# Attention's first pair: value gathers and next tables behind the rotations, and ScalarE for the roots of the first rotations

## The chip, the cores and the metric

The kernel runs on one core of a Trainium2 chip. The metric is the device time of one execution in microseconds (us). The kernel before takes 3504.65 us, the median of 3 runs (3504.32 to 3507.08). In the profile, PE is TensorE's matrix work, PEld its weight loads, DVE is VectorE, ACT is ScalarE, POOL is GpSimd, and SP is the engine from whose queue most DMAs start.

## The reference, cut to what matters

The program is a network of four stages over 64 sequences of 32 tokens with 512 features, in float32: 2048 rows, which the kernel holds as 16 tiles of 128 rows. Each stage adds its result to `x`. The change lies in the third, an attention with cached keys and values (32 query heads, 8 key heads, 128 features per head, pages of 32 positions, 16 pages per sequence):

```python
def _rmsnorm(t, w):
    var = jnp.mean(t * t, axis=-1, keepdims=True)
    return t * jax.lax.rsqrt(var + EPS) * w

def _rope(t, pos):
    ...
    t1, t2 = (t[..., :D // 2], t[..., D // 2:])
    return jnp.concatenate([t1 * cos - t2 * sin, t2 * cos + t1 * sin], axis=-1)
```

For each token, `x` is multiplied by `Wq`, `Wk` and `Wv`; the heads of q and k go through `_rmsnorm` and `_rope`; the scores of q against the 512 cached keys and the sequence's own 32 are masked by the sequence's length, put through a softmax and multiplied with the values; `Wo` brings the result back to 512 features. What the change touches is the norm's factor `rsqrt(mean(t*t) + EPS)` and the rotation of the first tiles, and the order in which cached values are fetched.

## The kernel before, in words

**Steps and pairs.** Attention (`attention`, from line 1015) goes in 32 steps: two halves of the heads (16 query heads and 4 key heads each), and 16 tiles in each half. Two steps make a pair, whose two tiles are projected together (`class Projections`), so there are 16 pairs. Of a pair there are three groups of products: g = 0 gives keys and values, g = 1 and 2 the queries. A group is 7 products of half the depth (`ORDER`, a scheme of Strassen's kind: sums of quarter blocks of `x` in `x_sums`, prepared sums of the weights), each accumulated in one of two PSUM buffers (`mm`). After products 1 and 5 of a group ScalarE copies the buffer out (line 1212); after the others VectorE adds it to a result (line 1220; lines 1222 and 1225 add once more). A buffer is free for the next product but one when that is done.

**A rotation.** Every finished key or query tile (128 rows x 4 heads x 128) goes through `rotated` (line 1123). ScalarE squares it (L1116), VectorE sums the squares (L1118) and scales the sums (L1119), GpSimd raises them to the power -0.5 (L130) into `rs`. Meanwhile VectorE writes the products of the swapped halves with the sine table into `swapped`, of which there are two buffers (L1130), and multiplies the tile by the cosine table (L1133). GpSimd adds the two (L1134), which frees the `swapped` buffer, and multiplies with `rs` (L1135). TensorE then transposes the tile (`turned`, L1055) through a single PSUM buffer `tq`, and ScalarE copies the transposed keys (`kT_own`, L1234) or queries (`qT`, L1238) out. I call the rotations of the first pair k0, k1, q0, q1 and so on, in the order of the work.

**Tables.** The cosine and sine tables are already multiplied with the norm's weight: `tables` (line 1168) has GpSimd make two products for each of the two tiles (L1173), so four for the keys and four for the queries of a pair.

**Scores and values.** For a sequence and a key head, TensorE makes the scores (L1342), VectorE masks them and finds the largest (L1347), ScalarE takes the exponential (L1349), VectorE the reciprocal of its sum (L1351), ScalarE scales the part of the own positions (L1352), VectorE the rest (L1354); TensorE transposes the weights (L1055), ScalarE copies them (L1360), and TensorE multiplies with the values (L1060, `po`). The cached values come in `load_values` (line 1083): four gathers on GpSimd's queue, of 128 rows of 2 KB each. Own values are copied by ScalarE, eight small copies for two sequences (L1093). Key pages and weights are ordered by SP, in a fixed order (`load_by`, line 99).

**What sets the order.** The order within a pair is written out by hand as 64 slots for `turned`, `product`, `tables`, `x_sums` and so on. Pair n calls the key tables of pair n+2 in slot 40, and the query tables of pair n+1 in slot 3. In the first pair the tables of the second pair are called in slots 7 and 10. Ahead of the first slot stands a prologue (lines 1461 to 1514), which does the first 21 products of pair 0 in portions, `products(4)`, `products(5)` and so on, with the key loads, own values, the gathers of the first sequences (`values_of(0)` and `values_of(HKP)`) and the first transposes between. A framework places each engine's instructions in a queue by priorities and data, so an instruction that has its data early can be moved ahead of others; `tc.issue_after(ins)` forces those issued inside it to stand behind `ins` on their engine. In the prologue of before, the gathers are forced to stand behind `p.last_pool`, the last of pair 0's own table products.

Of the kernel before, what the change touches and what calls it, by code (L numbers as in the profile page):

```python
# [27 lines left out]
AF = mybir.ActivationFunctionType  # L28
ALU = mybir.AluOpType
# [4 lines left out]
P = 128  # L34
# [9 lines left out]
HQ, HK, HD = 32, 8, 128  # L44
# [5 lines left out]
REP = HQ // HK  # L50
# [964 lines left out]
def attention(c, known, x_in, y_part, y_out, sums, tail):  # L1015
# [15 lines left out]
    tc, nc, a = c.tc, c.nc, c.a  # L1031
    half = HD // 2
    n_c = L // P
    with ExitStack() as outer:
# [8 lines left out]
        cos, sin, rows, lens = known.cos, known.sin, known.rows, known.lens  # L1043
        norm, keys = known.norm, known.keys
# [52 lines left out]
        soon = []  # L1097
# [22 lines left out]
            c.inverse_root(rs, REP)  # L1120
            return rs

        def rotated(t, tab):

            src = t.rearrange("p (h d) -> p h d", d=HD)
            ct, st = tab
            rs = squares_and_root(src)
            tmp = wk.tile([P, REP, HD], F32, name="swapped", bufs=2)
            for lo, hi in ((0, half), (half, 0)):
                nc.vector.tensor_tensor(  # L1130
                    tmp[:, :, lo:lo + half], src[:, :, hi:hi + half],
                    st[:, lo:lo + half].unsqueeze(1).to_broadcast([P, REP, half]), ALU.mult)
            nc.vector.tensor_tensor(src, src, ct.unsqueeze(1).to_broadcast([P, REP, HD]), ALU.mult)  # L1133
            nc.gpsimd.tensor_tensor(src, src, tmp, ALU.add)  # L1134
            nc.gpsimd.tensor_tensor(src, src, rs.unsqueeze(2).to_broadcast([P, REP, HD]), ALU.mult)  # L1135

        K2 = KC // 2

# [15 lines left out]
        class Projections:  # L1154
# [13 lines left out]
            def tables(self, n):  # L1168
                for i, T in enumerate(self.T):
                    ct = qp.tile([P, 2, half], F32, name=n + "_cos")  # L1170
                    st = qp.tile([P, 2, half], F32, name=n + "_sin")
                    for t, w_n, f in ((ct, norm[n][0], cos), (st, norm[n][1], sin)):
                        self.last_pool = nc.gpsimd.tensor_tensor(  # L1173
                            t, w_n, f[:, T, :].unsqueeze(1).to_broadcast([P, 2, half]), ALU.mult).ins
                    self.tabs[n, i] = tuple(t.rearrange("p u f -> p (u f)") for t in (ct, st))

            def x(self, i):
# [23 lines left out]
            def product(self, g, m):  # L1201
                (x11, x12), (_, x22) = self.blocks
                lhs = {1: x11, 2: x12, 3: self.s[3], 4: x22, 5: self.s[0], 6: self.s[1], 7: self.s[2]}[m]
                w = wps.pop(0)
                acc = ps.tile([P, D], F32, tag="mm", bufs=2, name="pq" if g else "pkv")
                part(acc, [(lhs[:, k, :], w[:, k, :]) for k in range(K2)], True, True)

                d = self.d = {} if m == 1 else self.d
                if m in (1, 5):
                    at = (0, 1) if m == 1 else (1, 1)  # L1210
                    d[at] = self.place(g, *at)
                    nc.scalar.copy(d[at], acc)
                    return
                if m == 2:
                    d[0, 0] = self.place(g, 0, 0)
                elif m == 6:
                    d[1, 0] = self.place(g, 1, 0)
                to, other = {2: ((0, 0), (0, 1)), 6: ((1, 0), (0, 1)), 3: ((0, 1), (1, 0)),
                             7: ((1, 0), (1, 0)), 4: ((1, 0), (1, 0))}[m]
                nc.vector.tensor_tensor(d[to], acc, d[other], ALU.add)  # L1220
                if m == 3:
                    nc.vector.tensor_tensor(d[0, 1], d[0, 1], d[1, 1], ALU.add)
                elif m == 7:
                    to = (1, 1)
                    nc.vector.tensor_tensor(d[1, 1], d[1, 1], d[1, 0], ALU.add)
                if m != 6 and not (g == 0 and to[1]):
                    soon.append(partial(rotated, d[to], self.tabs["q" if g else "k", to[0]]))

            def turned(self, g, i, n):
                r = self.c.pop((g, i, n)).rearrange("p (h d) -> p h d", d=HD)  # L1230
# [183 lines left out]
        projections = [Projections(n) for n in range(len(steps) // 2)]  # L1414
# [9 lines left out]
        def values_of(i):  # L1424
            if i < len(turns):
                s, h, b, _ = of(i)
                load_values(h, b)
# [33 lines left out]
        p = projections[0]  # L1461
# [11 lines left out]
        def products(n):  # L1473

            for i in range(count[0], count[0] + n):
                p.product(i // 7, p.ORDER[i % 7])
                if i >= 7 and p.ORDER[i % 7] in (7, 4):
                    held.extend(soon)
                    del soon[:]
                the_rest()  # L1480
                if i < 3 * 7 - 8 or i >= 3 * 7 - 4:
                    next_wp()
            count[0] += n
# [6 lines left out]
        for i in (0, HKP):  # L1490
            own_values_of(i)
        products(5)
        with tc.issue_after(p.last_pool):
            values_of(0)
        new_keys(0, 1)
        p.turned(0, 0, 0)
        load_keys(0, 1, range(2))
# [2 lines left out]
        p.turned(0, 1, 0)  # L1500
        products(1)
        p.turned(1, 0, 0)
        products(1)
        load_keys(0, 1, range(2, 4))
        start(0)
# [1 line left out]
        p.turned(1, 0, 1)  # L1507
        products(2)
        start(1)
        with tc.issue_after(p.last_pool):  # L1510
            values_of(HKP)
        projections[1].load()
        products(1)
# [12 lines left out]
        for s, (h, T) in enumerate(steps):  # L1526
# [3 lines left out]
            n = s // 2  # L1530
# [599 lines left out]
```

## Time and profile before

| what | value |
|---|---|
| time, median of 3 runs | 3504.65 us (3504.32 to 3507.08) |
| the profiled execution's own time | 3513.04 us |
| its span on the core | 3511.2 us |
| granted TensorE clock, mean | 0.991 |
| TensorE time in 1200 to 3160 us | 1957.04 of 1960 us |
| L1134, GpSimd add in the rotation | 160 times, 1301 ns each |
| L130, GpSimd power | 160 times, 1125 ns each |
| L1135, GpSimd product with the root | 160 times, 1078 ns each |
| L1086, gathers on GpSimd's queue | 512 times, 1009 ns each |
| L1173, table products on GpSimd | 128 times, 0.44 to 0.97 us each |

The profile is of one execution. Its times run from the start of the span; attention's first products start shortly before 1000 us, its first slots at about 1042 us, and after the first pairs one pair takes about 142 us. A line of a timeline gives the start, the duration, the engine and line, what is written and read, and in brackets how long the engine was idle before and what ended that. In a table of windows each column is an engine's busy time in the stretch, then the granted clock of TensorE (1.00 is full speed), the share of the DMA engines' time and the GB/s.

### The profile page before, as it was taken

The numbers are of one execution on the slowest core, as the hardware profiler recorded it, in microseconds if no ns is written. First come the engines' busy times: TensorE is split into PE (matmuls) and PEld (weight loads), VectorE is DVE, ScalarE is ACT, GpSimd is POOL, SyncE is SP. The second block draws the span as 40 slices with busy tenths as digits, with TensorE's granted clock in tenths as the row PEclk, the third lists the DMA queues.
The fourth block names the chain that finished last, engine by engine and source line by source line (L and its number), as shares of the span: only waits on it lengthen the run. The fifth ranks groups of instructions, "written<-read, shape, count | busy, mean of one in ns | idle before, by whom it ended". The sixth has DMA issues, their size and how long they took to land. (4 is left out here: it accounts for less than half of the span.)

```text
span 3511.2 us, 66971 instructions
## 1 busy us (share of the span) xinstructions
PE 3429.1 (98%) x21124; PEld 2690.3 (77%) x21124; DVE 2186.3 (62%) x5429; ACT 1627.0 (46%) x4259; POOL 1650.5 (47%) x1650
## 2 busy tenths in 40 slices
PE   8999999999989999999999999999999999999988
PEld 6556888888857777778777787787777877778776
DVE  5454444444357676776766767767677676675555
ACT  5332222222226555555555555555555555556322
POOL 0112433333257565655646556556565574554222
PEclk9999999999999999999999999999999999999989
DMA  5013645454467778788887888878878888878511
GB/s 207 25 52 125 195 154 176 156 165 154 142 225 233 238 258 260 251 261 252 258 260 251 253 257 255 264 245 262 268 250 269 257 262 263 255 235 250 187 59 43
DMA packets 631936, 740.26 MB, mean 211 GB/s; under 512 B 64546, under 2 KB 480290, under 8 KB 631586
## 3 DMA queue, kind: packets, MB, share of 16 engines
q1 hardware_dynamic: 580130, 562.94, 51.3%
q0 software_dynamic: 51456, 173.05, 14.1%
q8 instruction: 171, 2.80, 0.3%
q14 instruction: 179, 1.47, 0.1%
HBM read 689.61 MB, written 46.14 MB: 210 GB/s over the span
## 5 line engine op out<-in xcount | busy, mean ns | idle before, releaser
L1086 POOL DMA_INDIRECT vt<-in_v_rows,v_rows x512 | 516.4, 1009 | 300.9 <-PE po L1060 175.6
L1349 ACT ACTIVATE pr<-pr,low 128x544 f32<-128x544 f32 x512 | 383.3, 749 | 546.9 <-DVE low L1347 544.9
L1342 PE MATMUL sc<-kt,qT 128*128 128x288 f32 (+1 forms) x2048 | 554.7, 393 | 8.7 <-DVE low L1347 5.4
L1342 PEld LDWEIGHTS sc<-kt,qT 128*128 128x128 f32 x2048 | 384.9, 190 | 223.7 <-issue 121.0
L1060 PEld LDWEIGHTS po<-prT,vt 128*128 128x128 f32 x4096 | 522.7, 192 | 33.4 <-ACT prT L1360 13.8
L1060 PE MATMUL po<-prT,vt 128*128 128x128 f32 x4096 | 544.3, 276 | 3.5 <-ACT prT L1360 2.0
L1347 DVE CUSTOM_DVE_ANT_0 pr<-sc,mask 128x544 f32<-128x544 f32 x512 | 368.1, 719 | 140.7 <-PE sc L1342 140.1
L1134 POOL TENSOR_TENSOR projected<-projected,swapped 128x512 f32<-128x512 f32 x160 | 208.2, 1301 | 303.1 <-DVE projected L1133 278.3
L1354 DVE TENSOR_SCALAR pr<-pr,low 128x512 f32<-128x512 f32 x512 | 317.1, 619 | 12.8
L1055 PE MATMUL prT_ps<-ident,pr 128*128 128x128 f32 x2048 | 312.1, 275 | 1.6 <-DVE pr L1354 1.5
L1360 ACT COPY prT<-prT_ps 128x512 f32<-128x512 f32 x512 | 294.0, 574 | 32.6 <-PE prT_ps L1055 25.2
L1351 DVE RECIPROCAL low<-low 128x1 f32<-128x1 f32 x512 | 81.9, 160 | 318.4 <-ACT pr L1349 318.0
L1055 PEld LDWEIGHTS prT_ps<-ident,pr 128*128 128x128 f32 x2048 | 237.7, 142 | 10.9 <-issue 2.9
L1060 PE MATMUL py<-wo,oT 128*128 128x256 f32 x1024 | 243.5, 381 | 0.0
L1060 PE MATMUL pq<-wp,x_sums 128*128 128x512 f32 x512 | 240.5, 593 | 0.1
L1060 PEld LDWEIGHTS py<-wo,oT 128*128 128x128 f32 x1024 | 187.5, 191 | 21.5
L130 POOL TENSOR_TENSOR rs<-rs,minus_half 128x4 f32<-128x4 f32 x160 | 180.0, 1125 | 22.2 <-DVE low L1351 14.6
L1060 PE MATMUL pq<-wp,xT 128*128 128x512 f32 x384 | 183.7, 602 | 5.0 <-DVE projected L1220 5.0
L1060 PE MATMUL py<-wo,o_sum 128*128 128x256 f32 x768 | 182.9, 382 | 3.0 <-DVE o_sum L1278 2.1
L1352 ACT ACTIVATE own_pr<-pr,low 128x32 f32<-128x32 f32 x512 | 164.9, 322 | 44.1 <-DVE low L1351 41.0
L1093 ACT COPY own_vt<-v 32x128 f32<-32x128 f32 x512 | 150.8, 295 | 55.1 <-PE po L1060 42.4
L1135 POOL TENSOR_TENSOR projected<-projected,rs 128x512 f32<-128x512 f32 x160 | 172.6, 1078 | 7.9
(348 smaller groups left out, 6477.6 us busy)
## 6 DMA issues: line engine op xcount, KB each, us to landing
kt<-in_kT SPq DMA_DIRECT2D x2048, 64.0 KB
wp<-in_sums SPq DMA_DIRECT2D x192, 512.0 KB
wo<-out_sums SPq DMA_DIRECT2D x128, 512.0 KB
wp<-in_WqT SPq DMA_DIRECT2D x96, 512.0 KB
wo<-in_WoT SPq DMA_DIRECT2D x96, 512.0 KB
down1T<-in_down1T SPq DMA_DIRECT2D x80, 256.0 KB
wp<-in_WkT SPq DMA_DIRECT2D x32, 512.0 KB
xt<-x SPq DMA_DIRECT2D x48, 256.0 KB
```

The lines of the kernel that those rows point to most:

```text
L130: self.nc.gpsimd.tensor_tensor(t, t, self.minus_half[:, :n], ALU.pow)
L1055: c.on_pe(nc.tensor.transpose(pt[:, m, :], piece, c.ident))
L1060: c.on_pe(nc.tensor.matmul(out, lhsT, rhs, start=first and i == 0, stop=last and i == len(pairs) - 1))
L1086: nc.gpsimd.indirect_dma_start(out=vts[b % 2][:, n, :], out_offset=None, in_=a["v_rows"], in_offset=bass.IndirectOffsetOnAxis(ap=rows[h][: ...
L1134: nc.gpsimd.tensor_tensor(src, src, tmp, ALU.add)
L1135: nc.gpsimd.tensor_tensor(src, src, rs.unsqueeze(2).to_broadcast([P, REP, HD]), ALU.mult)
L1342: c.on_pe(nc.tensor.matmul(sc[:, lo + n * PSIZE:lo + m * PSIZE].rearrange("p (n k) -> p n k", k=PSIZE), q, kt[:, n:m, g, :], start=True, s ...
L1347: nc.vector.tensor_tensor_reduce(pr[:, :NK], sc[:, lo:lo + NK], masks[h, b], -SCALE, 3.0e38, ALU.add, ALU.min, low[:, 0:1])
L1349: nc.scalar.activation(pr[:, :NK], pr[:, :NK], AF.Exp, bias=low[:, 0:1], scale=-1.0, accum_out=low[:, 1:2])
L1352: nc.scalar.activation(own_prs[b % 2][:, g * S:(g + 1) * S], pr[:, L:NK], AF.Copy, scale=low[:, 2:3])
L1354: nc.vector.tensor_scalar(pr[:, :L], pr[:, :L], low[:, 2:3], None, ALU.mult)
L1360: last_prT.append(nc.scalar.copy(prT, pt).ins)
```

## The change

The change has four parts, all in `attention`:

1. `rotated` keeps the instruction of its GpSimd add (L1134 of before) in a list `last_turn`.
2. It gets a switch `by_scalar`. With it, the product with the root is done by ScalarE, in four products of 128x128, one for each head, instead of one GpSimd product of 128x512. It is set in the first pair alone, for the keys' two rotations and the first two of the queries, four in all.
3. `tables` no longer records `last_pool`. Its products are forced to stand behind the last L1134 that was written so far, if there is one. This holds for the tables of all pairs but the first.
4. In the prologue the first gathers, `values_of(0)`, move from after 14 products to behind the third transpose, and are forced to stand behind the last L1134 so far, the fifth of the pair, instead of behind pair 0's tables. The gathers of the second sequence, `values_of(HKP)`, stay in their place in the code, and are forced to stand behind the last L1134 there, the sixth.

```diff
+        last_turn = []
+
-        def rotated(t, tab):
+        def rotated(t, tab, by_scalar=False):
...
-            nc.gpsimd.tensor_tensor(src, src, tmp, ALU.add)
-            nc.gpsimd.tensor_tensor(src, src, rs.unsqueeze(2).to_broadcast([P, REP, HD]), ALU.mult)
+            last_turn.append(nc.gpsimd.tensor_tensor(src, src, tmp, ALU.add).ins)
+            if by_scalar:
+                for h in range(REP):
+                    nc.scalar.activation(src[:, h, :], src[:, h, :], AF.Copy, scale=rs[:, h:h + 1])
+            else:
+                nc.gpsimd.tensor_tensor(src, src, rs.unsqueeze(2).to_broadcast([P, REP, HD]), ALU.mult)
...
-                    for t, w_n, f in ((ct, norm[n][0], cos), (st, norm[n][1], sin)):
-                        self.last_pool = nc.gpsimd.tensor_tensor(
-                            t, w_n, f[:, T, :].unsqueeze(1).to_broadcast([P, 2, half]), ALU.mult).ins
+                    with tc.issue_after(last_turn[-1]) if last_turn else nullcontext():
+                        for t, w_n, f in ((ct, norm[n][0], cos), (st, norm[n][1], sin)):
+                            nc.gpsimd.tensor_tensor(
+                                t, w_n, f[:, T, :].unsqueeze(1).to_broadcast([P, 2, half]), ALU.mult)
...
-                    soon.append(partial(rotated, d[to], self.tabs["q" if g else "k", to[0]]))
+                    soon.append(partial(rotated, d[to], self.tabs["q" if g else "k", to[0]],
+                                        self is projections[0] and (g == 0 or g == 1 and m in (2, 3))))
...
         products(5)
-        with tc.issue_after(p.last_pool):
-            values_of(0)
         new_keys(0, 1)
...
         p.turned(1, 0, 0)
+        with tc.issue_after(last_turn[-1]):
+            values_of(0)
         products(1)
...
-        with tc.issue_after(p.last_pool):
+        with tc.issue_after(last_turn[-1]):
             values_of(HKP)
```

In the built program TensorE's and SP's queues are the same as before. On ScalarE's queue the four products of k0 stand ahead of the own-value copies; those of k1 stand behind the copy of the 8th product and ahead of the squares of q0 and the copy of the 10th product; those of q0 and q1 follow with the squares of q1 between them, and behind them come the copy of the first transposed keys and that of the 15th product. On GpSimd's queue pair 0's tables are followed by the first rotations at once; the first gathers stand behind the fifth L1134, between the work of the fifth and sixth rotation. In the later pairs the four products of the key tables stand together behind an L1134 of the queries, later in the queue than before, and the query tables stand around the sums `x_sums` and `o_sum`.

## What the change does to the time: the prediction

> **What bounds the kernel now.** I read the busy times of section 1 first:
>
> ```profile
> PE 3429.1 (98%) x21124; PEld 2690.3 (77%) x21124; DVE 2186.3 (62%) x5429; ACT 1627.0 (46%) x4259; POOL 1650.5 (47%) x1650
> ```
>
> TensorE is busy for 98% of the span, so an edit on another engine counts only where TensorE waits for it. The change edits GpSimd's and ScalarE's queues, so I went to TensorE's timeline in attention's first pair. The columns are start, duration, instructions, and in brackets the idle time before and what ended it:
>
> ```profile
> 1018.74 0.60 PE L1055 MATMUL qkT_ps<-ident,projected 128*128 128x128 f32 x4
> 1024.31 3.78 PE L1060 MATMUL pq<-wp,xT 128*128 128x512 f32 x4 [4.96 <-DVE projected L1220]
> 1027.88 1.06 PE L1055 MATMUL qkT_ps<-ident,projected 128*128 128x128 f32 x4
> ...
> 1045.90 0.66 PE L1055 MATMUL qkT_ps<-ident,projected 128*128 128x128 f32 x4 [0.56 <-POOL projected L1135]
> ```
>
> The 15th product waits 4.96 us for VectorE to evacuate the 13th (two PSUM buffers). VectorE's timeline tells why that is late:
>
> ```profile
> 1019.39 0.76 DVE L1130 TENSOR_TENSOR swapped<-projected,q_sin 128x256 f32<-128x256 f32 x2 [2.39 <-POOL projected L1134]
> 1020.07 0.68 DVE L1118 TENSOR_REDUCE rs<-squares 128x4 f32<-128x512 f32 x1
> 1020.67 2.91 DVE L1133 TENSOR_TENSOR projected<-projected,q_cos 128x512 f32<-128x512 f32 x1
> ...
> 1023.57 0.68 DVE L1220 TENSOR_TENSOR projected<-pq,projected 128x512 f32<-128x512 f32 x1
> ```
>
> The fourth rotation (q1) needs a `swapped` buffer that the second (k1) gives back with GpSimd's L1134 at 1018.11. GpSimd's timeline shows gathers and tables of the next pair ahead of it:
>
> ```profile
> 1015.64 0.95 POOL L1086 DMA_INDIRECT vt<-in_v_rows,v_rows  x1 [0.30 <-issue]
> 1016.60 0.71 POOL L1173 TENSOR_TENSOR k_cos<-k_norm_row,cos 128x128 f32<-128x128 f32 x1
> 1017.28 0.86 POOL L1173 TENSOR_TENSOR k_sin<-k_norm_swapped,sin 128x128 f32<-128x128 f32 x2
> 1018.11 1.25 POOL L1134 TENSOR_TENSOR projected<-projected,swapped 128x512 f32<-128x512 f32 x1
> ```
>
> Then L1133 takes 2.91 us instead of the 0.68 of the same line at 1008.63, ending as GpSimd's L1135 and L1134 end: the two engines seem to keep each other from the same memory. The windows (TensorE, its loads, VectorE, ScalarE, GpSimd, granted clock, DMA share, GB/s) give the rest of the price:
>
> ```profile
> 1022.80:1029.60 6.80, 5.29 (x10) 2.61 (x11) 4.36 (x7) 1.17 (x2) 6.24 (x6) 0.50 0.74 244
> 1159.30:1162.70 3.40, 3.40 (x12) 2.44 (x12) 2.21 (x7) 2.00 (x5) 2.52 (x3) 0.50 0.87 311
> 1264.00:1292.00 28.00, 27.90 (x157) 20.75 (x156) 23.05 (x52) 16.07 (x43) 22.03 (x20) 1.00 0.81 260
> ```
>
> After the stall 5.29 us of TensorE's work runs at half clock, which loses 2.65. **At stake in the first pair: 4.96 + 2.65 = 7.6 us.**
>
> **First pair: what leaves and what comes.** Eight gathers (0.94 to 1.26 us and 0.30 between each) and the next pair's tables leave the stretch ahead of the first four rotations. The 7.6 us go. GpSimd's L1134 for k0 then starts when its first tables end (1002.56), is done at 1003.8, and the root (L130, 1.05 to 1.26) at about 1005.0.
>
> For four rotations L1135 (1.03 to 1.35) becomes four ScalarE products of 128x128, which the trace of before does not have. The nearest rows are L1352, a ScalarE product with the same kind of scale on 128x32, at 0.32, and a ScalarE copy of 128x512 at 0.59. Four of them cost between 1.28 and 2.36; I take 1.3, nearer the first row in size. Their sum is small; their place is not. ScalarE's queue is in order, and I walked it with row durations (times after 1000):
>
> - products k0 5.2 to 6.5; behind them the own-value copies (2.45 us) to 8.95, squares k1 (0.63), and the copy (0.59) that evacuates the 8th product, to 10.2 instead of 8.86. TensorE's 10th product is about 0.5 late.
> - k1: VectorE's reduction and scale end near 11.0, GpSimd's L1134 and root take to 13.4, the products of k1 to 14.7, squares of q0 to 15.3, and only then comes the copy that evacuates the 10th product: 15.85 instead of 12.30. TensorE's 12th product needs that buffer: **a stall of 2.2 us** that before did not have.
> - q0 and q1 go through VectorE, GpSimd and ScalarE one behind the other. The evacuation of the 13th product ends near 22.9, a stall of 0.5 to 1.45 (I take 1.0), and the 15th product starts at 23 to 24.5, no earlier than about 24.31.
> - the copy of the first transposed keys stands behind the products of q1 (24.7 to 26.0) and frees the PSUM buffer of the second: their transposes start at 26.6 to 28.2, a stall of 1.2 to 2.4 (I take 2.2).
>
> Clock: in before, the half clock came after stalls of 1.69 and 2.04 us (at 1157.45 and 1055.54) too, for 3.4 us, as in the window at 1159.30; after the stall of 1.06 at 1173.62 it did not come. So two stalls of about 2.2 cost 1.7 each. Sum: 2.2 + 1.7 + 1.0 + 2.2 + 1.7 = 8.8, less the 7.6 that go, **+1.2**. Ends: -2.0 (0.5 and 1.2 for the uncertain stalls, no clock loss after the last), +4 (products at 0.59 delay two of these waits by 1.1 each).
>
> [...]
>
> **Gathers behind rotations.** The four first gathers now stand among the fifth and sixth rotation's GpSimd work, the others behind the sixth's L1134. At 1045.90 TensorE already waits 0.56 for L1135; one gather more (0.95 + 0.30) ahead of such a product adds between 0 and 2.5 (two), and I take **+1.1**. The data themselves are not late: the first product with values is at 1046.39, and the gathers of before, issued from 1002.72 to 1015.64, had all landed by 1023.1; the DMA share of the stretch was 0.74 to 0.84.
>
> **All later pairs.** The new order is attached to every call of `tables`, not just the first. In before GpSimd does the four key products of pair n+2 at 1192 to 1197 and 1227 to 1232, where it idles (8.94 of 15 us busy; 4.22 of the next 20). Now they stand in a cluster behind a query rotation of slot 40 and after, at about 1264 to 1292. There GpSimd is busy 22.0 of 28 us, VectorE 23.05, TensorE 27.90 (the window above). The four products take 1.8 to 2.3 us (0.45 to 0.97 each). Fourteen pairs have such a cluster. A gain from the emptied stretch is excluded: TensorE is busy 15.00 of 15 us there. What it costs lies between 0 (VectorE gets at the memory between two GpSimd operations, TensorE doesn't notice) and 2.2 (VectorE held through two operations, as L1133 at 1020.67), or 14 x 2.2 = 31, more with clock. The nearest row is in that same stretch: L1354 at 1275.85 took 1.07 instead of 0.49 beside L1135, 0.6 lost. 14 x 0.6 = **+8.4**. The query tables move among sums with little around them; I count 0.
>
> Sum: +1.2 + 1.1 + 8.4 = +10.7. On the profiled execution (3513.04; 3511.2 span and 1.84 around it) that is 3523.7; it lay 8.4 above the median, so on the median 3504.65 + 10.7 = **3515**.
>
> **Rivals.**
> A, even: VectorE mostly gets its turn between two operations, the clusters cost 0.2 each or less (3), and the first pair breaks even: 3504 to 3511, say 3507. For it: VectorE is 62% busy, and where I looked at GpSimd operations that follow each other without a gap, VectorE came in between 19 times and went on waiting 14 times. Against: the stretch is the fullest of the pair.
> B, faster: ScalarE's products do not hold up an evacuation copy. Place: the copy of the 10th product, which must end by about 1013.6; it decides whether 2.5 us of my walk are wrong, for instance if L130 runs shorter without gathers beside it. Then the 7.6 go and little comes: 3497. Against: the chain reduce, L1134, L130, products, squares is five engine changes long, and all its durations are from rows.
> C, worse: each cluster holds VectorE 1.5 us, and in half of the pairs the clock falls (0.85 each): 14 x 2.35 = 33, 3538. Against: stalls of 1.06 in before left the clock alone.
> That the change does not act as told is excluded for the first pair: the built queues show the gathers behind the rotations; it is the tables that do more than told.
>
> **Numbers.** Forecast 0.48 (3508 to 3526 with its own bounds; 0.06 of it under 3511.7), A 0.30, B 0.08, C 0.14. 0.2% is 7 us, about what a measurement of this kernel can tell from no change. Faster 0.08, within 0.36 (A and the 0.06), slower 0.56. The range reaches from the lower end of the first pair with hidden tables (-2, and half way to B) to 14 x 2.2 = +31: 3500 to 3536; B and most of C's upper half, under 0.2, stay out.
>
> **What the profile after would show.** Right: no wait of 4.96 for the 13th product's evacuation; ScalarE's copy of the 10th product at about 1015 behind products and squares, and TensorE waiting about 2 us for it; in each pair a group of four table products inside 1264 to 1292 with VectorE operations stretched there and new TensorE waits of 0.3 to 1 us. Wrong: TensorE without idle time between the 10th and 15th product (B), or TensorE's sum from 1200 to 3160 unchanged at 1957 of 1960 and the steady pairs no longer than 142.3 us (A). If the key tables stand elsewhere in time than I put them, the main term falls.

## The result and the profile after

The changed kernel takes 3537.09 us, the median of 4 runs (3534.69 to 3542.39), against 3505.86 of the kernel before (3504.32 to 3509.31, 4 runs): a ratio of 1.009 with a 95% interval from 1.0072 to 1.0107, so 25 to 37 us slower. The two profiled executions lie 24.8 us apart (3537.84 and 3513.04). The forecast was 3515 with a range from 3500 to 3536. The direction was right and the size was not: about a third of the loss was seen coming, and the range ended 1 us short.

Section 1 of the page after has a longer span (3536.0) for the same work. VectorE's busy time grew most, by 8.0 us for the same 5429 instructions; ScalarE has 16 products more and GpSimd 4 fewer:

```profile
PE 3431.5 (97%) x21124; PEld 2689.7 (76%) x21124; DVE 2194.3 (62%) x5429; ACT 1630.4 (46%) x4275; POOL 1650.5 (47%) x1646
```

Where in time does the loss lie? The 512 exponentials of the scores stand in the same order in both kernels, so I compared the start of the first of each pair, after less before, in the two traces: -2.3 us in the first pair, then +1.3, +1.6, +3.8, +5.8, +7.7, +9.7, +11.7, +13.7 and on to +25.6 in the fifteenth pair and +26.8 in the last. The first products gained 2.3 (0.3 of it stood ahead of attention's first `x_sums` already), the rest of the first pair lost 3.6, the second 0.3, and then **every pair from the third to the fourteenth lost about 2.0 us** (2.2 in the third); the fifteenth, which has no key tables to make, lost 1.2. In 1200 to 3160 us TensorE was busy for 1935.91 us, where it had been busy for 1957.04.

TensorE's timeline of the first pair, after (line numbers are 2 to 8 higher than before, L1134 is L1136, L1135 is L1141, L1234 is L1242):

```profile
1015.43 5.40 PE L1060 MATMUL pq<-wp,x_sums 128*128 128x512 f32 x8 [1.96 <-ACT projected L1219]
1020.67 1.88 PE L1060 MATMUL pq<-wp,xT 128*128 128x512 f32 x4
1022.38 0.60 PE L1055 MATMUL qkT_ps<-ident,projected 128*128 128x128 f32 x4
1022.82 1.88 PE L1060 MATMUL pq<-wp,xT 128*128 128x512 f32 x4
1026.40 0.63 PE L1055 MATMUL qkT_ps<-ident,projected 128*128 128x128 f32 x4 [1.70 <-ACT kT_own L1242]
...
1045.73 1.12 PE L1055 MATMUL qkT_ps<-ident,projected 128*128 128x128 f32 x4 [2.70 <-POOL projected L1141]
```

The wait of 4.96 before the 15th product (now at 1022.82) is gone. In its place are the two waits at ScalarE's copies that the walk through ScalarE's queue had, 1.96 (forecast 2.2) and 1.70 (2.2), and the wait at the sixth rotation grew from 0.56 to 2.70. ScalarE's timeline shows the copy of the 10th product behind the four products of k1 and the squares of q0:

```profile
1013.12 1.28 ACT L1139 ACTIVATE projected<-projected,rs 128x128 f32<-128x128 f32 x4 [3.40 <-POOL rs L130]
1014.30 0.61 ACT L1116 ACTIVATE squares<-projected 128x512 f32<-128x512 f32 x1
1014.82 0.56 ACT L1219 COPY projected<-pq 128x512 f32<-128x512 f32 x1
```

And GpSimd's timeline shows the gather between the sum and the product of the sixth rotation, behind the late gathers of the first sequence:

```profile
1040.53 1.28 POOL L1136 TENSOR_TENSOR projected<-projected,swapped 128x512 f32<-128x512 f32 x1
1041.76 1.52 POOL L130 TENSOR_TENSOR rs<-rs,minus_half 128x4 f32<-128x4 f32 x1
1043.47 1.12 POOL L1086 DMA_INDIRECT vt<-in_v_rows,v_rows  x1 [0.19 <-issue]
1044.63 1.05 POOL L1141 TENSOR_TENSOR projected<-projected,rs 128x512 f32<-128x512 f32 x1
```

In the later pairs the 2.0 us come at two places. The larger one was not in the forecast. In the sixth pair TensorE waits once for VectorE's L1362 (L1354 of before), which stands behind the mask operation:

```profile
1768.40 0.63 PE L1055 MATMUL prT_ps<-ident,pr 128*128 128x128 f32 x4 [1.12 <-DVE pr L1362]
```

VectorE's mask operation, after:

```profile
1763.42 4.24 DVE L1342 TENSOR_SCALAR mask<-keys,lens_f 128x544 f32<-128x544 f32 x1
...
1767.77 0.49 DVE L1362 TENSOR_SCALAR pr<-pr,low 128x512 f32<-128x512 f32 x1
```

GpSimd beside it, after:

```profile
1761.03 2.37 POOL L1286 TENSOR_TENSOR o_sum<-oT 128x1024 f32<-128x1024 f32 x1
1763.35 0.47 POOL L1180 TENSOR_TENSOR q_cos<-q_norm_row,cos 128x128 f32<-128x128 f32 x1
1763.78 2.34 POOL L1287 TENSOR_TENSOR oT<-oT 128x1024 f32<-128x1024 f32 x1
1766.09 0.45 POOL L1180 TENSOR_TENSOR q_sin<-q_norm_swapped,sin 128x128 f32<-128x128 f32 x1
1766.50 0.44 POOL L1180 TENSOR_TENSOR q_cos<-q_norm_row,cos 128x128 f32<-128x128 f32 x1
1766.91 0.44 POOL L1180 TENSOR_TENSOR q_sin<-q_norm_swapped,sin 128x128 f32<-128x128 f32 x1
```

The same place in before, VectorE, then GpSimd's last operation there, then TensorE:

```profile
1755.67 3.01 DVE L1334 TENSOR_SCALAR mask<-keys,lens_f 128x544 f32<-128x544 f32 x1
...
1758.79 0.49 DVE L1354 TENSOR_SCALAR pr<-pr,low 128x512 f32<-128x512 f32 x1
```

```profile
1756.03 2.34 POOL L1279 TENSOR_TENSOR oT<-oT 128x1024 f32<-128x1024 f32 x1
```

```profile
1759.42 0.63 PE L1055 MATMUL prT_ps<-ident,pr 128*128 128x128 f32 x4
```

An operation that takes 0.49 us alone is busy for 3.01 in before, and ends 0.31 us after GpSimd's L1279. In after three table products follow that line without a gap, three times 0.41; the mask operation ends 0.31 us after the last of them and has taken 1.23 more. The same lengths recur: 3.00 to 3.02 us in 12 pairs of before, 4.23 to 4.24 in 13 pairs of after. Before, TensorE just bridged it: L1354 ended at 1759.28, 0.14 us ahead of the transposes that read its result. After, they wait 1.12.

The other place is the stretch of the key tables at 1842 to 1855 in the same pair. It adds 0.74 us per pair, near the 0.6 of the forecast, but not in the way that the forecast had it. VectorE in after:

```profile
1844.53 1.83 DVE L1132 TENSOR_TENSOR swapped<-projected,q_sin 128x256 f32<-128x256 f32 x2
...
1852.46 2.13 DVE L1362 TENSOR_SCALAR pr<-pr,low 128x512 f32<-128x512 f32 x1
```

GpSimd in after:

```profile
1845.45 0.63 POOL L1180 TENSOR_TENSOR k_cos<-k_norm_row,cos 128x128 f32<-128x128 f32 x1
1846.04 0.64 POOL L1180 TENSOR_TENSOR k_sin<-k_norm_swapped,sin 128x128 f32<-128x128 f32 x1
...
1852.01 1.05 POOL L130 TENSOR_TENSOR rs<-rs,minus_half 128x4 f32<-128x4 f32 x1
1853.04 1.26 POOL L1136 TENSOR_TENSOR projected<-projected,swapped 128x512 f32<-128x512 f32 x1
```

The same L1362 and L130 in before (L1354 there):

```profile
1844.04 1.07 DVE L1354 TENSOR_SCALAR pr<-pr,low 128x512 f32<-128x512 f32 x1
```

```profile
1841.13 1.05 POOL L130 TENSOR_TENSOR rs<-rs,minus_half 128x4 f32<-128x4 f32 x1
```

Beside the table products VectorE's L1132 took 1.83 us instead of 0.98, which made the next exponential 0.64 late; but TensorE did not wait there, and the exponential behind it was back in time. The lasting loss comes some 8 us later. At this place after runs 8.98 us behind before, yet L130 of the next rotation comes 10.88 later, since GpSimd had the four table products to do ahead of its gathers. So L1362, which in before began during that rotation's L1135 and took 1.07, now begins with L130 and is busy until 0.29 us after L1136 ends. TensorE then waits 0.44 us at 1858.43 for VectorE's L1355, and that exponential is 0.75 late for good. All 12 pairs from the third to the fourteenth show these two steps. The view by source of after shows which VectorE operations were drawn out like this (ns: shortest, median, longest):

```profile
L1355 DVE CUSTOM_DVE_ANT_0 pr<-sc,mask x512: 706/718/726, 1031.9 to 3303.2; 128x544 f32<-128x544 f32 x171
L1118 DVE TENSOR_REDUCE rs<-squares x160: 668/680/687, 1000.2 to 3191.6; 128x4 f32<-128x512 f32 x160
L1227 DVE TENSOR_TENSOR projected<-pq,projected x160: 672/684/693, 1010.6 to 3184.8; 128x512 f32<-128x512 f32 x160
L1362 DVE TENSOR_SCALAR pr<-pr,low x512: 469/487/3926, 1033.7 to 3305.3; 128x512 f32<-128x512 f32 x171
L1342 DVE TENSOR_SCALAR mask<-keys,lens_f x128: 489/497/4242, 994.3 to 3273.9; 128x544 f32<-128x544 f32 x128
```

The first three, which read PSUM or reduce, stay within 21 ns. The products of a tile with a scalar, with medians of 487 and 497 ns, reach 3926 and 4242, over eight times as long.

### The profile page after: what moved, and what is told of

It is laid out like the page before. It is cut to its first block, busy times and chain, and to the rows that moved or that the text cites. A ratio compares the mean times of both kernels' runs of the same rounds, so it can differ in the third digit from the quotient of the medians.

```text
span 3536.0 us, 66985 instructions
## 1 busy us (share of the span) xinstructions
PE 3431.5 (97%) x21124; PEld 2689.7 (76%) x21124; DVE 2194.3 (62%) x5429; ACT 1630.4 (46%) x4275; POOL 1650.5 (47%) x1646
## 5 line engine op out<-in xcount | busy, mean ns | idle before, releaser
L1086 POOL DMA_INDIRECT vt<-in_v_rows,v_rows x512 | 527.4, 1030 | 309.0 <-PE po L1060 183.6
L1355 DVE CUSTOM_DVE_ANT_0 pr<-sc,mask 128x544 f32<-128x544 f32 x512 | 368.0, 719 | 141.9 <-PE sc L1350 141.5
L1136 POOL TENSOR_TENSOR projected<-projected,swapped 128x512 f32<-128x512 f32 x160 | 208.1, 1301 | 412.7 <-DVE projected L1135 372.8
L1362 DVE TENSOR_SCALAR pr<-pr,low 128x512 f32<-128x512 f32 x512 | 307.3, 600 | 12.8
L130 POOL TENSOR_TENSOR rs<-rs,minus_half 128x4 f32<-128x4 f32 x160 | 186.8, 1167 | 209.2 <-DVE low L1359 203.3
L1141 POOL TENSOR_TENSOR projected<-projected,rs 128x512 f32<-128x512 f32 x156 | 167.7, 1075 | 8.6
```

The lines of the kernel that those rows point to most:

```text
L130: self.nc.gpsimd.tensor_tensor(t, t, self.minus_half[:, :n], ALU.pow)
L1086: nc.gpsimd.indirect_dma_start(out=vts[b % 2][:, n, :], out_offset=None, in_=a["v_rows"], in_offset=bass.IndirectOffsetOnAxis(ap=rows[h][: ...
L1136: last_turn.append(nc.gpsimd.tensor_tensor(src, src, tmp, ALU.add).ins)
L1355: nc.vector.tensor_tensor_reduce(pr[:, :NK], sc[:, lo:lo + NK], masks[h, b], -SCALE, 3.0e38, ALU.add, ALU.min, low[:, 0:1])
L1362: nc.vector.tensor_scalar(pr[:, :L], pr[:, :L], low[:, 2:3], None, ALU.mult)
```

## The experiments

Theory 1 is that the forced order of the tables in the later pairs is the loss, because GpSimd operations without gaps between them keep a VectorE operation waiting. Its rivals: the first pair's new order shifts all that follows (theory 2); the key tables are the price and the query tables cost nothing, as the prediction had it (theory 3); the price is the place in GpSimd's queue (theory 4); being forced costs wherever it is (theory 5). e1 to e4 ran on one chip, e5 to e8 on a second and e9 to e12 on a third, each beside the kernel before, whose median was 3517.13 on the first, 3515.59 on the second and 3508.92 on the third; so runs are compared by the ratio to before, and, for single microseconds, by the steps in their traces.

| run | median us | ratio to before, 95% interval | step per later pair, us |
|---|---|---|---|
| e1_tables_first_only | 3518.86 | 1.0008 (0.9999 to 1.0017) | 0.0 to 0.1 |
| e2_tables_only | 3539.65 | 1.0065 (1.0051 to 1.0079) | 2.0 |
| e3_query_tables | 3535.01 | 1.0051 (1.0038 to 1.0065) | 1.2 |
| e4_key_tables | 3528.84 | 1.0035 (1.0021 to 1.0048) | 0.75 |
| e5_no_scalar | 3514.97 | 0.9996 (0.9987 to 1.0004) | 0.0 |
| e6_scalar_only | 3520.20 | 1.0013 (1.0005 to 1.0022) | 0.0 |
| e7_gathers_later | 3513.99 | 0.9997 (0.9988 to 1.0006) | 0.0 |
| e8_gathers_later_no_scalar | 3509.22 | 0.9985 (0.9976 to 0.9994) | 0.0 |
| e9_query_tables_twice | 3569.04 | 1.0170 (1.0151 to 1.0189) | 4.5 |
| e10_query_tables_elsewhere | 3510.64 | 1.0007 (0.9997 to 1.0016) | +0.1 to -0.5 |
| e11_gathers_alone | 3501.32 | 0.9982 (0.9973 to 0.9991) | 0.0 |
| e12_scalar_behind_copies | 3504.11 | 0.9985 (0.9976 to 0.9994) | 0.0 |

The step is taken as above, from the third pair on, by the first exponential of each pair against the trace of before; two pairs of e1 and one each of e8 and e9 are 0.6 to 1.7 off.

### The forced tables, whole and in halves

e1, on the changed kernel:

```diff
-                    with tc.issue_after(last_turn[-1]) if last_turn else nullcontext():
+                    with tc.issue_after(last_turn[-1]) if last_turn and (self is projections[1]) else nullcontext():
```

> The change with one part taken back: the tables are forced behind a rotation for the second pair alone; from the third pair on GpSimd may do them early, as before the change. Theory 1 (the forced order of the later pairs' tables is the whole loss, 2.0 us per pair from the third pair on; the first pair gains 2.3 at the products and loses 3.6 at the gathers): this run stands 1 to 4 us over the kernel before, about 3507, and the steps per pair are those of before. Theory 2 (the first pair's new order shifts the phase of the later pairs' queues, and the tables merely ride along): it stays near the changed kernel, 3530 to 3537, with the 2.0 us per pair.

e2, on the kernel before, with `last_turn` filled as in the change and nothing else of it:

```diff
+                    with tc.issue_after(last_turn[-1]) if last_turn and self is not projections[1] else nullcontext():
-                    for t, w_n, f in ((ct, norm[n][0], cos), (st, norm[n][1], sin)):
+                        for t, w_n, f in ((ct, norm[n][0], cos), (st, norm[n][1], sin)):
...
```

> The kernel before with the forced order of the tables from the third pair on as its only edit; gathers and the products with the roots as before. Theory 1: it loses the 2.0 us per pair alone, 13 to 14 times, so +25 to +29 over the kernel before. Theory 2: nothing, within 3 us of the kernel before.

e3 and e4 are e1 with `(self is projections[1] or n == "q")` and `(self is projections[1] or n == "k")` as the condition.

> The change, but from the third pair on only the query tables are forced behind a rotation; the key tables are free. Theory 1, split by the trace after (1.25 us per pair at the sums of the previous pair's output, where three query products now follow the second sum without a gap): 14 times 1.25, so +17 over the run with the tables of the second pair alone. Theory 3 (as the prediction had it: the key tables are the price, the query tables cost nothing): within 2 us of that run.

> The change, but from the third pair on only the key tables are forced behind a rotation; the query tables are free. Theory 1: 14 times 0.74 (the second step of the trace after in each pair), so +10 over the run with the tables of the second pair alone. Theory 3: all of the loss, +25 to +28.

e1 lies 1.7 us over before (1 to 4 were expected) and e2 22.5 over it, a little under the 25 to 29 that were expected; its trace has the same 2.0 us in each pair. The forced order alone makes the loss, and taking it back ends it. Theory 2 is out. Over e1, e3 costs 16.2 us and e4 10.0 (expected 17 and 10). Theory 3 is out too: the query tables, which the prediction counted at nothing, are the larger part.

### How the tables cost: their number and their neighbours

e9, on e3 (`twice` is 2 for the forced query tables, else 1):

```diff
-                        for t, w_n, f in ((ct, norm[n][0], cos), (st, norm[n][1], sin)):
+                        for t, w_n, f in ((ct, norm[n][0], cos), (st, norm[n][1], sin)) * twice:
```

> As the run with only the query tables forced from the third pair on, but each of these four GpSimd products is done twice, one after the other, with the same values: four products of 0.44 us more in the same place. Theory 1 (VectorE's mask operation is held until GpSimd's unbroken run of operations ends): the mask operation takes 1.7 us longer again (about 5.9 us instead of 4.2), TensorE's wait behind it grows from 1.1 to about 2.9, and each pair costs 1.75 more, with a half clock behind it up to 3.4 more: +24 to +48 over the run with the query tables once. Theory 4 (the price is the place in GpSimd's queue: work behind the tables comes late): GpSimd idles 3.7 us behind them in the trace after, so four products more cost nothing.

e10, on e3:

```diff
-                        at(3, partial(p.tables, "q"))
+                        at(16, partial(p.tables, "q"))
```

> As the run with only the query tables forced from the third pair on, but they are called in slot 16 instead of slot 3, and so stand behind the sum of the first key rotation instead of behind the two sums of the output. Theory 1: what costs is the neighbour; away from the two long sums the mask operation is held no longer than in the kernel before (3.0 us), the wait of 1.1 us at it goes, and most of the 1.2 us per pair with it, so +0 to +6 over the run with the tables of the second pair alone. Theory 5 (being forced, or being late, is what costs, wherever): still +14 to +17.

e9: VectorE's mask operation, and the first and last GpSimd operations of the run beside it that follow the second sum:

```profile
1773.69 5.87 DVE L1343 TENSOR_SCALAR mask<-keys,lens_f 128x544 f32<-128x544 f32 x1
```

```profile
1776.35 0.45 POOL L1181 TENSOR_TENSOR q_sin<-q_norm_swapped,sin 128x128 f32<-128x128 f32 x1
...
1778.82 0.44 POOL L1181 TENSOR_TENSOR q_sin<-q_norm_swapped,sin 128x128 f32<-128x128 f32 x1
```

TensorE behind it, and the two windows (TensorE, its loads, VectorE, ScalarE, GpSimd, clock, DMA share, GB/s):

```profile
1780.31 0.63 PE L1055 MATMUL prT_ps<-ident,pr 128*128 128x128 f32 x4 [2.77 <-DVE pr L1363]
```

```profile
1777.40:1780.80 3.40, 0.63 (x7) 0.52 (x6) 3.32 (x4) 0.33 (x2) 1.86 (x5) 1.00 0.68 200
1780.90:1784.20 3.30, 3.30 (x10) 2.67 (x9) 3.29 (x9) 2.21 (x6) 1.26 (x2) 0.50 0.69 200
```

Four products more draw the mask operation out by 1.63 us (5.87 against 4.24), and it again ends 0.3 us behind the last of them; all 13 pairs have 5.87 or 5.88. TensorE's wait grows by 1.65, which now brings a half clock of 3.4 us in nearly every pair: 4.5 us per pair, 60 over before and some 42 more than e3. Theory 4, by which four products ahead of 3.7 idle us would cost nothing, is out.

e10, VectorE at the same place, and GpSimd's second sum there:

```profile
1758.82 0.49 DVE L1342 TENSOR_SCALAR mask<-keys,lens_f 128x544 f32<-128x544 f32 x1
...
1759.44 2.37 DVE L1362 TENSOR_SCALAR pr<-pr,low 128x512 f32<-128x512 f32 x1
```

```profile
1758.88 2.64 POOL L1287 TENSOR_TENSOR oT<-oT 128x1024 f32<-128x1024 f32 x1
```

Without a table between the two sums, the mask operation begins in a gap of GpSimd of 0.08 us and takes 0.49; now GpSimd's sum is the one that takes 0.3 longer, and L1362 is held until 0.29 us after it. All 13 pairs have a mask operation of 0.49. TensorE has no wait there. All four query products stand behind the sum of a key rotation instead (1767.98 to 1770.86), as forced as in e3 and 6 to 9 us later in the pair, and the loss is gone. Theory 5 is out. **The cause of the larger part of the later pairs' loss is shown: query products added to GpSimd's run of sums, through which VectorE's mask operation waits.** That the key tables cost the smaller part is shown by e4; how they do it (the next rotation comes late and meets L1362) is read from the traces of after and e4, and no run moved them elsewhere.

Which lines vary, the view by source of after shows: L1362 and L1342 take up to 3.93 and 4.24 us, L1355 and L1227, which have an input in PSUM, at most 0.73 and 0.69. That the two engines keep each other from the same memory, as the prediction has it, was my reading of ends that coincide; no run here shows what VectorE waits for.

That the mask operation waits through every boundary between GpSimd's sums and tables is what the three lengths 3.01, 4.24 and 5.87 show. It is no rule for every run without gaps: of the 51 L1362 of after that take over 0.65 us, 26 end 0.28 to 0.30 us behind a GpSimd operation whose successor has already begun, and L1132 at 1844.53 ends 0.28 us behind the `k_cos` product at 1845.45, while the `k_sin` product follows it without a gap. What decides whether VectorE gets in stays open.

### The first pair: ScalarE and the gathers

e5 is e1 with the switch off; e6 is the kernel before with `by_scalar` and its switch as the only edit:

```diff
-                                        self is projections[0] and (g == 0 or g == 1 and m in (2, 3))))
+                                        False))
```

> The change with the tables forced in the second pair alone, and all products with the roots back on GpSimd. If ScalarE's queue is what the new stalls of the first products wait for (copies of the 10th product and of the first transposed keys behind the products with the roots: 1.96 and 1.70 to 1.98 us, and a half clock), both go, and no stall over 1 us is left before the scores: about 4 us less than with ScalarE's products. If GpSimd's queue was the bottleneck all along, as the change would have it, the wait for VectorE's evacuation of the 13th product comes back in part, 2 to 4 us. The wait of 2.2 to 2.7 us at the sixth rotation, behind a gather, stays in both cases.

> The kernel before with the roots of the first four rotations multiplied by ScalarE as its only edit; gathers and tables as before. If the products only take work off GpSimd: the stall of 4.96 us shrinks by up to 2 us (two products of 1.05 us leave GpSimd's queue ahead of the late rotation). If ScalarE's queue in order is what counts: the roots come late on GpSimd (1010.2 and 1020.4 in the profile of before, behind the gathers), and the own-value copies and the evacuation copies of the 8th and 10th product stand behind them: stalls of some 5 us each, 5 to 12 us slower than before.

e7 is e1, and e8 is e5, with the gathers moved; `last_of` holds the last GpSimd instruction of each rotation (the root, L130, where ScalarE multiplies, else L1141). e11 is e8 with no table forced.

```diff
-        with tc.issue_after(last_turn[-1]):
+        with tc.issue_after(last_of[3]):
             values_of(0)
...
-        with tc.issue_after(last_turn[-1]):
+        with tc.issue_after(last_of[5]):
             values_of(HKP)
```

> The change with the tables forced in the second pair alone, and the gathers forced elsewhere: the first four behind the root of the fourth rotation, where GpSimd idles 7 us in the trace after, the others behind the whole of the sixth rotation instead of behind its sum. If one gather between the sum and the product of the sixth rotation, and the lateness that the first four hand on, make the wait of 2.2 to 2.7 us and its half clock: the wait falls to the 0.6 us of before, 3 to 4 us less than the run with the tables of the second pair alone, so 1 to 2 us under the kernel before. If it is ScalarE or the first products that make it: no change.

> The gathers as in the run before this one, and all products with the roots on GpSimd (the first four gathers behind the whole of the fourth rotation); tables forced in the second pair alone. If both waits are as told, this loses the stalls at ScalarE's copies and the wait at the sixth rotation: the first 32 groups of scores 6 to 8 us shorter than in the kernel before, so about 7 us (0.2%) faster. If GpSimd's queue is the bound of the first products, it is no better than the run with ScalarE's products and later gathers.

> The gathers behind the whole of the fourth and the sixth rotation, products with the roots on GpSimd, and no table forced at all: the move of the gathers alone. If the tables of the second pair, which then stand between the first rotations again (some 2 us of GpSimd), matter beside the gathers (8 times 1.25 us), the stall before the 15th product comes back to 2 or 3 us, and it is 2 to 4 us slower than the run with later gathers and the tables forced in the second pair. If the gathers were nearly all of it, the two are within 1.5 us.

e12 is e7 with ScalarE's products called later, k0 and k1 after 14 products and q0 and q1 after the first transpose, each forced behind the last copy of L1212 or L1234 that is written so far:

```diff
-                for h in range(REP):
-                    nc.scalar.activation(src[:, h, :], src[:, h, :], AF.Copy, scale=rs[:, h:h + 1])
+                by_roots.append(partial(times_root, src, rs))
...
+        def times_root(src, rs):
+            with tc.issue_after(last_copy[-1]):
+                for h in range(REP):
+                    nc.scalar.activation(src[:, h, :], src[:, h, :], AF.Copy, scale=rs[:, h:h + 1])
```

> Later gathers, tables forced in the second pair alone, and ScalarE's products with the roots forced behind the copies that TensorE waits for: those of k0 and k1 behind the evacuation of the 10th product, those of q0 and q1 behind the copy of the first transposed keys. If ScalarE's order, not its work, makes the waits of 1.96 and 1.9 us: the first goes, the second shrinks to under 1 us, and the scores start as early as in the run without ScalarE's products, or up to 1 us earlier, since GpSimd has 4 us less to do. If the chain of engines is the cause: no better than the run with later gathers and ScalarE's products.

By the traces, from GpSimd's first `x_sums` of the first pair to the first exponential, and to that of the second pair:

| kernel | to the first scores, us | to the second pair's scores, us |
|---|---|---|
| before | 39.5 | 178.1 |
| after | 37.5 | 179.8 |
| e1 | 39.2 | 183.9 |
| e5 | 32.6 | 179.7 |
| e6 | 43.5 | 180.9 |
| e7 | 37.7 | 175.9 |
| e8 | 32.6 | 174.0 |
| e11 | 32.6 | 169.2 |
| e12 | 32.6 | 171.0 |

*ScalarE's order.* e6 has the 10th product waiting 6.15 us for the copy of the 8th, since the products of k0 ahead of that copy start at 1010.27 only, when GpSimd is through with the first five gathers and the rotation behind them; it was slower by 4.6 us in the median, just under the 5 to 12 of the second reading of its expectation. e5 and e8, without ScalarE's products, reach the scores 5 to 7 us earlier than their pairs e1 and e7. e12 has the products and is as early as e8, since those of k0 and k1 no longer stand ahead of a copy (in this kernel L1130 is ScalarE's product and L1227 the copy, L1212 of before):

```profile
1012.20 0.58 ACT L1227 COPY projected<-pq 128x512 f32<-128x512 f32 x1 [0.29 <-PE pq L1060]
1012.68 2.44 ACT L1130 ACTIVATE projected<-projected,rs 128x128 f32<-128x128 f32 x8
```

The products of q1 still stand ahead of two copies, and TensorE waits 0.40 us there. So the order on ScalarE is what cost, not the 1.28 us of four products. In right order they bring no more than GpSimd's own products do (e12 and e8 both 0.9985). On whole executions the step is small: without the products e5 lies 0.12% below e1, and e8 0.12% below e7, and the intervals overlap in both cases.

*The gathers.* Counted from the first `x_sums`, e7 and e8 start the first gathers 9 to 11 us earlier than the change, in a stretch where GpSimd was idle, and put the others behind the sixth rotation's product: the wait of 2.2 to 2.7 us there falls to 0.3 and its half clock goes. e7 lies 1.6 us under before, as expected (1 to 2), and e8 6.4 (about 7 expected), though its trace reaches the second pair's scores only 4.1 us earlier than before, and not 6 to 8. e11, TensorE, at the two old waits (L1229 is L1220 of before, L1142 is L1135):

```profile
1020.86 1.98 PE L1060 MATMUL pq<-wp,xT 128*128 128x512 f32 x4 [1.09 <-DVE projected L1229]
...
1039.85 0.66 PE L1055 MATMUL qkT_ps<-ident,projected 128*128 128x128 f32 x4 [0.56 <-POOL projected L1142]
```

*The second pair's tables.* By the ratios e11 and e8 are alike (0.9982 and 0.9985), as the second reading of e11's expectation had it: the move of the gathers is nearly all of the gain, and the stall before the 15th product stays at 1.09 us with the four key products back between the rotations. With intervals 6 us wide the runs can't say more. The traces do: forcing the second pair's tables cost time. In after all eight of them stand at 1070 to 1080, where in before they are spread from 1016 to 1073, and from the ninth exponential to the fourteenth (1071 to 1097) after loses 1.6 us against before. In that stretch e1, e3, e5, e8, e9, e10 and e12 lose 2.0, e4 1.6 and e7 0.8; e2, e6 and e11, which leave these tables free, lose 0.0. e8 and e11 differ in this one edit. By the second pair's scores e11 is 4.8 us ahead of e8, 2.0 of it here and some 1.7 by a half clock that only e8 has (1151.4 to 1154.8). e11 is the best kernel of the study, 7.6 us under before in the median; its interval overlaps those of e8 and e12.

What stays open: why the whole change reaches the second pair's scores 4 us earlier than e1, though e1 forces fewer tables. It leads by 1.7 us at the first scores already, and gains 2.4 more between 1097 and some 1160 us, with smaller gains and losses elsewhere; no run separates the waits there. The half clocks don't explain it: in attention, up to the second pair's scores, both traces have four windows of it.

## Why the prediction was wrong

- *The first products.* The 7.6 us went, as forecast. Of the waits that came instead, ScalarE's two were there with 1.96 and 1.70 for 2.2 each; the third (1.0, before the 15th product) was absent, and one half clock came rather than two. Net -2.3 measured (-2.0 from the first `x_sums` on), +1.2 forecast, with -2.0 as the lower end. The mechanism held, shown by e5, e6 and e12.
- *The gathers behind rotations.* Forecast +1.1 within 0 and 2.5; measured +4.7, from the first exponential to the ninth. The wait grew by 2.14 where I took 1.1, and a half clock followed (1044.2 to 1051.0, with 5.27 us of work at half speed, 2.6 lost), which I had priced for ScalarE's waits and not for this one. e7 shows that it was the gathers' place.
- *The second pair's tables.* I counted them only as leaving the first rotations. Where they landed, at 1070 to 1080, they cost 1.6 us; e8 against e11 shows it.
- *Luck in the first pair.* Together it came to +1.3, near the forecast +2.3, but by terms that were each off and cancelled: -2.3, +4.7, +1.6, and -2.7 later on, most of it because the half clock of before at 1159.3 did not come.
- *The key tables.* 0.6 per pair forecast, 0.74 to 0.75 measured: 10.0 us in e4 against 8.4. The size was near; the path was another one, and so it was partly luck. The forecast had VectorE held beside the tables, and took its price from an L1354 that was drawn out in before already. What VectorE lost beside the tables (0.64) TensorE bridged. The loss came because GpSimd's next rotation began 1.9 us late, and the same L1354 was then held through two of its operations.
- *The query tables: the step that failed.* "The query tables move among sums with little around them; I count 0." They cost 1.2 per pair, 16.2 us in e3, and are the greater part of the miss. I looked at the stretch where the key tables were going and not at the one where the query tables were. A mask operation of 3.01 us for 0.49 stood there in the profile of before, ending with GpSimd's sum; it said that VectorE waited there until GpSimd's sum had ended, and that products added behind the sum could be paid by VectorE in full, as e3 and e9 then showed. That TensorE would notice could be read from the 0.14 us of slack behind it.
- *The range.* Its upper end, +31, was the bound of the key tables alone. With the same bound for the query tables it would have held the result.
- *Rivals.* A (hidden) and B (faster) did not occur; C's size came about, by another mechanism: neither 1.5 us in the key cluster (0.75) nor a lower clock (the clock stood at 1.00 through 1200 to 3160 us).

## What to carry to other kernels

When an edit forces an order in a helper that all iterations call, price each place where its instructions land, by the neighbours there, and not just the place that the edit was made for. Look in the old profile for an operation that takes several times its shortest duration: here the mask operation, 3.01 us for 0.49, marked a place where VectorE already waited for GpSimd. Three query products more, 1.23 us, lengthened it by 1.23, and TensorE waited 1.12 once the slack of 0.14 us behind it was used up. Look behind the place too: the key tables cost nothing beside them and 0.75 us at the next rotation. An engine's queue with waits in it is no place for helpful work ahead of a copy that frees a buffer: in after TensorE waited 1.96 and 1.70 us for copies behind ScalarE's products, and in e12, where those of k0, k1 and q0 stand behind copies, 0.40 once.

## What the runs showed of the hardware

- VectorE's two products of a tile with a scalar, L1342 and L1362 of after, take 0.49 and 0.47 us at the shortest. Those that took over 0.65 us, 16 and 51, each ended 0.28 to 0.31 us behind the end of a GpSimd operation. Beside sums and table products the mask operation waited through all of them: 3.01 us in before, 4.24 in after, 5.87 in e9. In e10 it got in at a gap of 0.08 us, and GpSimd's operation was 0.3 longer (2.64 for 2.34). Elsewhere VectorE got in between two operations without a gap (26 of the 51 L1362 in after).
- The half clock of before starts at 1022.8, 1056.9 and 1159.3 between 1000 and 1200 us and lasts 6.8, 3.4 and 3.4 us; the starts are 34.1 and 102.4 apart, 10 and 30 times 3.41. In after it starts at 1016.9, 1044.2 and 1057.8 there, 8 and 4 times 3.41 apart. In the 3.4 us ahead of these starts TensorE was busy for 0.00, 1.20 and 1.69 us in before, 1.44, 1.30 and 1.45 in after. Windows of after, TensorE's busy time first:

```profile
1013.40:1016.80 3.40, 1.44 (x4) 0.68 (x4) 1.85 (x4) 1.98 (x6) 0.49 (x1) 1.00 1.06 377
1016.90:1020.20 3.30, 3.30 (x5) 1.30 (x4) 2.10 (x5) 1.61 (x5) 1.65 (x2) 0.50 0.67 166
1023.70:1027.10 3.40, 1.70 (x8) 0.86 (x7) 1.05 (x3) 2.26 (x7) 0.78 (x1) 1.00 0.71 228
1027.10:1030.50 3.40, 3.40 (x12) 1.72 (x11) 1.54 (x4) 1.67 (x3) 0.00 (x0) 1.00 0.29 80
```

And of e9:

```profile
2217.77:2221.18 3.41, 1.41 (x9) 1.36 (x10) 3.27 (x6) 0.95 (x2) 0.96 (x3) 1.00 0.53 149
2221.18:2224.59 3.41, 3.41 (x23) 3.09 (x23) 3.12 (x10) 1.94 (x6) 2.18 (x3) 1.00 0.73 203
```

The first window of after, 1.44 of 3.40 us busy, was followed by half clock, and so was one of before with 1.69 (1155.9 to 1159.3); the third of after, with 1.70, was not, and neither was that of e9, with 1.41. So no one share parts these cases: between 1.4 and 1.7 us both occur. Nor does the length of one wait. In after the wait of 1.96 us had 3.4 us of half clock behind it, by my estimate 1.7 lost (half of 3.4), and that of 1.70 had none. The same wait for VectorE at the end of the first pair was 1.69 us in before, all but 0.15 of it inside one window, with a half clock behind it; it was 1.71 in after, across two windows (2.52 and 2.41 us busy), with none. What decides is not shown.
